# Two graph-attention layers on one core: k and q of layer 1 return together, and x is loaded later

## The chip, the cores and the metric

The kernel runs on one NeuronCore of a Trainium2 chip. TensorE (PE) multiplies matrices, VectorE (DVE), ScalarE (ACT) and GpSimd (POOL) do the elementwise work, and SyncE (SP) issues nearly all DMA transfers. The metric is the device time of one execution in microseconds; less is better. Nothing is split over cores, so the slowest core is the only core.

## The reference, cut to what matters

x is (128, 128, 512): 128 graphs of 128 nodes with 512 features; adj is a boolean mask (128, 128, 128). Two attention layers follow each other, each with a residual sum and a layer norm without scale. Layer 0 has 4 heads of 64, layer 1 has 8 heads of 64, a layer norm of its own input, and a mask in which every node also sees itself. All is float32.

```python
# layer 0
q, k, v = (split_heads(x @ W) for W in (Wq, Wk, Wv))            # 4 heads x 64
sim  = where(adj[:, None], einsum('bhid,bhjd->bhij', q, k) * scale, -finfo.max)
attn = softmax(sim)
x = layernorm(x + einsum('bhij,bhjd->bhid', attn, v) @ Wo + bo)
# layer 1
h = (x - mu) * rsqrt(var + 1e-5) * gamma + beta
q, k, v = split(h @ w_qkv.T)                                     # 8 heads x 64
scores = where(mask | eye, einsum('bihd,bjhd->bhij', q, k) * SCALE, -1e9)
out = einsum('bhij,bjhd->bihd', softmax(scores), v) @ w_out.T + b_out
x = layernorm(x + out)
```

## The kernel before

The 128 graphs are taken in 64 groups of two (`G = 2`). The function `step(s)` runs for s = 2 to 63; before it stands `opening()`, after it `closing_a`, `closing_b` (twice) and `last`. One step works on several groups at once: the projections of layer 0 for group s (`product_0`), the scores and softmax of layer 0 for group s-1 (part 0), attention and output of layer 0 for group s-2, the q, k and v of layer 1 for group s-3 (`qk`, `v`), scores and softmax of layer 1 for group s-4 (parts 1 and 2, one for each graph of the group), and attention and output of layer 1 for group s-5. Each matrix product is done in seven block products in place of eight (the numbers 1 to 7 in `product`, `product_0` and `out_product`), whose sums and differences DVE, ACT and POOL make.

The order on each engine is the order of the calls in `step`: the schedule is written by hand. Every engine takes its instructions in that order and waits in front of each one until its data and its buffer are ready. SP does the same with DMA transfers: a transfer that waits for something holds back all that were written after it.

Where a tile has to be transposed, DVE turns its blocks of 32 by 32 and the tile goes out to DRAM and comes back in four fetches (`fetch`, line 237), one for each quarter of the partitions, with the blocks in their new places. Five things take this way in each step:

- the normed rows of layer 0 on their way into layer 1: `turn` (store `scr`, line 234) and `arrive` (fetch into a tile with tag "raw"), read by ACT in `finish`;
- q and k of layer 0: `turn_qk0` (`scrqk`), `arrive_qk0` (`rawqk`); the q half is put in order by ACT in `q0_in_order` (line 277), and the k half is read by PE in the scores at line 562;
- the probabilities of each part: `blocks` (`scrp`, line 643) and `probs_arrive` (`pT`), read by PE in `attend` at line 691;
- k of layer 1: `taken_tokens` (lines 388 to 410). The half for the first graph comes from block product 2, the half for the second from product 4. Each is turned into the tile `tk`, which has one buffer, and stored at once (`scrk`, line 408). `k_arrive` fetches both halves into `kt`;
- q of layer 1: products 3 and 7 are turned into `tq`, which takes a turn of the tag "raw", and stored together (`scrq`, line 410). `q_arrive` fetches it into `rawq`, again with the tag "raw", and ACT puts it in order and scales it in `q_in_order` (line 435). PE reads `qo` and `kt` at line 568 in the next step.

Groups 0, 1 and the last three (`PLAIN_QK`) make q and k of layer 1 with the features on the partitions directly, and need no way through DRAM. The turned tiles of `turn`, `turn_qk0` and `blocks` share one tag "turned" with two buffers.

x is also loaded a second time, in a layout of 32-row quarters (`load_quarters`, four transfers, tile tag "x" with one buffer), which DVE turns in `transposed` (line 112). `load_ahead(s + 1)` (line 859) issues these four and the mask, near the beginning of the step; `arrive(s - 3)` follows it, and `flush()` issues, after ACT's layer norm, the store of the finished rows (`out_dram`, line 761).

The order of SP in one step of the steady part is therefore: x (4) and mask, raw (4), out, r, the stores of the probabilities of parts 0 and 1, scrqk, pT of parts 0 and 1 together (4), the first half of k, rawqk (4), the probabilities of part 2, q, the second half of k, rawq (4), kt (4), pT of part 2 (4), scr.

At the beginning, rows of the two weight matrices of layer 1 are loaded into tiles that are not used yet (`spare_rows`, lines 67 to 73), and transposed by PE.

Of the kernel before, what the change touches and what calls it, by code (L numbers as in the profile page):

```python
# [17 lines left out]
P = 128  # L18
D = 64
G = 2  # L20
# [7 lines left out]
def kernel(ctx: ExitStack, tc: tile.TileContext, x, adj, wq, wk, wv, wo, bo,  # L28
# [28 lines left out]
    def flush(what=later):  # L57
        while what:
            what.pop(0)()
# [7 lines left out]
    def spare_rows(pool, tag, n):  # L67
        rows_n = pool.tile([P, n, E], F32, tag=tag, name=f"raw_{tag}_{len(spare)}")
        spare.extend(rows_n[:, i] for i in range(n))

    for pool, tag, n in ((five, "r", 2), (five, "r", 2), (one, "kt", 2), (two, "v1", 2), (two, "v1", 2),
                         (one, "xT1", 2), (one, "aT1", 2), (one, "sm1", 2)):
        spare_rows(pool, tag, n)

    X, XT = {}, {}

    def load_rows(g):
        if 0 <= g < NG and g not in R:
            R[g] = five.tile([P, G, E], F32, tag="r", name=f"r_{g}")
            nc.sync.dma_start(R[g], x[g * G:(g + 1) * G].rearrange("b n e -> n b e"))  # L80
# [19 lines left out]
    def load_ahead(g):  # L100
        if g < NG:
            load_quarters(g)
            load_mask(g)
# [133 lines left out]
    def fetch(dst, scr):  # L237
        src = scr.rearrange("(a r) q x -> r q a x", r=32)
        for q in range(4):
            nc.sync.dma_start(dst[32 * q:32 * q + 32], src[:, q])  # L240
# [12 lines left out]
    def arrive(g):  # L253
        if not 0 <= g < NG:
            return
        RAW[1] = one.tile([P, 4, G, KC, 32], F32, tag="raw", name=f"raw_{g}")
        fetch(RAW[1].rearrange("p a b c i -> p a (b c i)"), SCR[1])

    PLAIN_0 = (0, 1, 2)
# [106 lines left out]
    def tap(kind, g, i, src, scale=1.0):  # L366
        EV[kind, i] = one.tile([P, 512], F32, tag=f"e{i}", name=f"e{kind}{i}_{g}")[:, :src.shape[1]]
        if scale == 1.0:
            nc.scalar.copy(EV[kind, i], src)  # L369
        else:  # L370
            nc.scalar.activation(EV[kind, i], src, AF.Copy, scale=scale)
# [11 lines left out]
        else:  # L383
            nc.vector.tensor_add(to, src, EV["v", e])

    QO, KT, TQ, SCRQ = {}, {}, {}, {}

    def taken_tokens(g, i, src):

        if i in (1, 5, 6):  # L390
            return tap("qk", g, i, src)
        if i == 4:
            done = src
        else:
            done = EV["qk", {2: 1, 3: 6, 7: 5}[i]]
            nc.vector.tensor_add(done, src, done)
        what, b = {2: ("k", 0), 7: ("q", 1), 3: ("q", 0), 4: ("k", 1)}[i]
        if i in (2, 7):
            SCRQ[what] = dram.tile([P, 4, G, K1 * 32], F32, tag=f"scr{what}", name=f"scr{what}_{g}")
        if i == 7:  # L400
            TQ[what] = one.tile([P, 4, G, K1 * 32], F32, tag="raw", name=f"tq_{g}")
        elif what == "k":
            TQ[what] = one.tile([P, 4, K1 * 32], F32, tag="tk", name=f"tk{b}_{g}")
        t = TQ[what] if what == "k" else TQ[what][:, :, b]
        nc.vector.transpose(t.rearrange("p q (c j) -> p q c j", j=32),
                            done.rearrange("p (c q j) -> p q c j", q=4, j=32))
        if what == "k":
            nc.sync.dma_start(SCRQ[what][:, :, b], t)
        elif i == 3:
            nc.sync.dma_start(SCRQ[what], TQ[what])  # L410

    def k_tile(g):
        KT[g] = one.tile([P, 4, G, K1, 32], F32, tag="kt", name=f"kt_{g}")
        return KT[g]

    def q_tile(g, b):
        QO[g, b] = one.tile([P, K1, N], F32, tag=f"qo{b}", name=f"qo{b}_{g}")
        return QO[g, b]

    def q_arrive(g):  # L420

        if 0 <= g < NG and g not in PLAIN_QK:
            RAW["q"] = one.tile([P, 4, G, K1, 32], F32, tag="raw", name=f"rawq_{g}")
            fetch(RAW["q"].rearrange("p a b c j -> p a (b c j)"), SCRQ["q"].rearrange("p q b x -> p q (b x)"))

    def k_arrive(g):

        if 0 <= g < NG and g not in PLAIN_QK:
            fetch(k_tile(g).rearrange("p a b c j -> p a (b c j)"), SCRQ["k"].rearrange("p q b x -> p q (b x)"))

    def q_in_order(g):

        if 0 <= g < NG and g not in PLAIN_QK:
            for b in range(G):
                nc.scalar.activation(q_tile(g, b).rearrange("p c (a j) -> p a c j", a=4), RAW["q"][:, :, b],
                                     AF.Copy, scale=SCALE)

    def plain_keys(g, b):
        return KT[g].rearrange("p a b c j -> p (a b c j)")[:, b * K1 * N:(b + 1) * K1 * N]

    def keys_of(g, b, kk, rows):
        if g in PLAIN_QK:
            return plain_keys(g, b).rearrange("p (c a j) -> p c a j", c=K1, a=4)[rows, kk]
        return KT[g][rows, :, b, kk]

    def taken_features(g, i, src):

        if i in (1, 5, 6):
            if i == 1:
                k_tile(g)  # L450
            return tap("qk", g, i, src, scale=SCALE if i != 1 else 1.0)
        if i == 2:
            nc.vector.tensor_add(plain_keys(g, 0), src, EV["qk", 1])
        elif i == 4:
            nc.scalar.copy(plain_keys(g, 1), src)
        else:
            b, e = {3: (0, 6), 7: (1, 5)}[i]
            nc.vector.scalar_tensor_tensor(q_tile(g, b).rearrange("p c n -> p (c n)"), src, SCALE,
                                           EV["qk", e], op0=ALU.mult, op1=ALU.add)
# [74 lines left out]


    SM, TOTAL, NMAX, PT, AT, SO = {}, {}, {}, {}, {}, {}
    K0, K1 = HEADS[0] // 2, HEADS[1] // 2
    PARTS = (0, 1, 2)

    def group_of(s, part):  # L540
# [3 lines left out]
    def scores(s, *parts):  # L544

        made = {}
        for part in parts or PARTS:
            g = group_of(s, part)
            if g is None:
                continue  # L550
            if part == 1:
                ps = [ps_st.tile([P, 512], F32, tag=t, name=f"sc{part}_{g}_{t}") for t in ("a0", "f0")]
            else:
                ps = [mm_tile(f"sc{part}_{g}_{i}") for i in range(2)]
            ps = [x.rearrange("p (k n) -> p k n", n=N) for x in ps]
            if part == 0:
                for b in range(G):
                    for h in range(HEADS[0]):
                        r = slice((h % 2) * D, (h % 2 + 1) * D)
                        k_ = (qkv0[r, b, h // 2, 2].rearrange("p (a j) -> p a j", j=32) if g in PLAIN_0 else  # L560
                              RAW[0][r, :, 1, b * K0 + h // 2])
                        nc.tensor.matmul(ps[h % 2][:, b * K0 + h // 2, :].rearrange("p (a j) -> p a j", j=32),  # L562
                                         qkv0[r, b, h // 2, 1], k_, start=True, stop=True)
            else:
                b = part - 1
                for h in range(HEADS[1]):
                    r = slice((h % 2) * D, (h % 2 + 1) * D)
                    nc.tensor.matmul(ps[h % 2][:, h // 2, :].rearrange("p (a j) -> p a j", j=32),  # L568
                                     QO[g, b][r, h // 2], keys_of(g, b, h // 2, r), start=True, stop=True)
            made[part] = ps  # L570
        return made

# [33 lines left out]
    def exps(s, part, *halves):  # L606
        if group_of(s, part) is None:
            return
        sm, nmax, total = SM[part], NMAX[part], TOTAL[part]
        for i in halves:  # L610
            for k in range(K1):
                nc.scalar.activation(sm[:, i, k, :], sm[:, i, k, :], AF.Exp, bias=nmax[:, i, k:k + 1],  # L612
                                     accum_out=total[:, i, k:k + 1])
# [193 lines left out]
    def qk(g, *which):  # L807
        for i in which:
            product("qk", g, i)
# [46 lines left out]
    def step(s):  # L856

        made = scores(s)
        load_ahead(s + 1)
        if s > 3:  # L860
            sums(0, s)
            arrive(s - 3)
        flush()
        load_rows(s - 1)
        masked(made, s, 0, 1, 2)
        if s == 3:
# [30 lines left out]
        product_0(s, 7)  # L897
        finish(s - 3, 1)
        exps(s, 2, 1)
        blocks(s, 1)  # L900
        product_0(s, 3)
        if s == 3:
# [9 lines left out]
            prepare(1)  # L912
        flush()
        if s > 2:
            probs_arrive(s, 0, 1)
        qk(s - 3, 2)
        arrive_qk0(s)
        blocks(s, 2)
        qk(s - 3, 6)
        if s == 3:  # L920
            weight_sums(w1v, wsv, 0)
# [7 lines left out]
        if s == 3:  # L929
            weight_sums(w1v, wsv, 1)  # L930
        qk(s - 3, 3, 4)
        q_arrive(s - 3)
        k_arrive(s - 3)
        probs_arrive(s, 2)
        out_product(1, s - 5, 1, 2)
        if s in (3, 4):
# [9 lines left out]
        out_product(1, s - 5, 6, 5)  # L946
        v(s - 3, 5)
        out_product(1, s - 5, 7, 3, 4)
        q_in_order(s - 3)
        q0_in_order(s)  # L950
        addend(0, s - 1)
        v(s - 3, 7)
        stats(1, s - 5, 0)
# [194 lines left out]
```

## Time and profile before

| | us |
|---|---|
| timed runs, median of 3 | 2765.82 (2763.13 to 2767.58) |
| the profiled execution | 2759.03 |
| its span, from the first to the last instruction | 2757.3 |
| median time from issue to landing: store of q (`scrq`) / half of k (`scrk`) | 5.0 / 5.8 |
| fetches of q (`rawq`) / k (`kt`), each of 128 KB | 2.9 / 3.5 |
| fetches of pT for two parts (256 KB) / for one (128 KB) | 5.2 / 3.9 |
| fetches of rawqk / of x | 6.1 / 5.0 |

The granted TensorE clock was 0.999 in the mean. DMA moved 562.73 MB in all, 204 GB/s in the mean. A page of a profile gives the busy time of each engine (PEld is the weight load of TensorE, which lies beside its matmuls), the same in 40 slices as tenths, and the groups of instructions with their mean duration. A wait is named by the engine that stood, its line and tile, and by what ended it. In the timeline a line is: start, duration, engine, line, operation, written tile <- read tiles, how many; and in brackets the idle time ahead of it and who ended it. SPq is SP's queue of DMA issues: the duration there is that of the issue, not of the transfer.

### The profile page before, as it was taken

The page shows a single profiled execution, that of the slowest core. Times are in us where ns is not written, and L with a number is a line of the kernel's source. Part 1 is how long each engine was busy: PE and PEld are TensorE (multiplying, and loading weights), DVE is VectorE, ACT ScalarE, POOL GpSimd, SP SyncE. Part 2 cuts the span into 40 slices and gives each one's busy share as a digit, 9 for nine tenths or more (in the row PEclk, how much of TensorE's full clock was granted, in tenths as well). Part 3 has the DMA queues.
Part 4 walks back from the last instruction along what each step waited for, and adds up shares of the span by engine and source line. Part 5 has one row for each costly group of instructions (what it writes and reads, how often), then busy time and mean ns, then how long its engine had stood idle before and what let it go on. Part 6 is the DMA issues. An engine that isn't in the chain of part 4 may idle for free.

```text
span 2757.3 us, 49223 instructions
## 1 busy us (share of the span) xinstructions
PE 2725.2 (99%) x15781; PEld 2024.6 (73%) x15781; DVE 2025.0 (73%) x3662; ACT 1510.6 (55%) x4805; POOL 1750.2 (63%) x2311
## 2 busy tenths in 40 slices
PE   8999999999999999999999999999999999999998
PEld 7867777677776677776776766777767767677787
DVE  5777777777777777777777777777777777777665
ACT  3465565564564655655645546556556465465554
POOL 4566666666666666666666666666666666666664
PEclk9999999999999999999999999999999999999999
DMA  6577878778778788787787787877877877878741
GB/s 171 151 196 211 220 205 222 209 205 225 214 202 227 202 215 218 206 220 213 202 228 209 208 224 203 218 212 207 225 207 207 225 206 214 219 204 222 204 126 62
DMA packets 525330, 562.73 MB, mean 204 GB/s; under 512 B 55304, under 2 KB 434192, under 8 KB 525072
## 3 DMA queue, kind: packets, MB, share of 16 engines
q1 hardware_dynamic: 524496, 559.05, 75.8%
q8 instruction: 127, 2.08, 0.3%
q14 instruction: 131, 1.07, 0.1%
q10 hardware_dynamic: 576, 0.52, 0.1%
HBM read 300.95 MB, written 258.47 MB: 203 GB/s over the span
## 4 chain that ended last, share of the span: by engine, by line
PE 89%; DMA 4%; ACT 3%; DVE 1%; POOL 1%; SPq 1%; issue 1%; ACTq 0%; POOLq 0%; DVEq 0%
PE qka L359 14%; PE a L490 11%; PE oa L528 11%; PE va L359 8%; PE qkf L359 7%; PE av L691 6%; PE of L528 6%; PE f L490 5%; PE vf L359 4%; PE qkc L359 4%; PE c L490 3%; PE oc L528 3%; PE sc L562 2%; PE sc L568 2%; PE vc L359 2%; DMA scrk<-tk 2%
## 5 line engine op out<-in xcount | busy, mean ns | idle before, releaser
L612 ACT ACTIVATE sm<-sm,nmax 128x128 f32<-128x128 f32 x1536 | 595.4, 393 | 7.6 <-DVE nmax L603 6.0
L621 POOL TENSOR_TENSOR sm<-sm,rec 128x1024 f32<-128x1024 f32 x192 | 364.1, 1896 | 360.5 <-DVE rec L620 357.6
L713 POOL TENSOR_TENSOR r<-r,bias 128x1024 f32<-128x1024 f32 x128 | 301.4, 2356 | 127.1 <-ACT r L712 127.1
L532 DVE TENSOR_TENSOR r<-oa,r 128x256 f32<-128x256 f32 x508 | 211.5, 416 | 159.8 <-PE oa L528 126.0
L612 ACT ACTIVATION_READ_ACCUMULATOR sm<-sm,nmax 128x1 f32 x1536 | 295.4, 192 | 0.0
L369 ACT COPY ev<-va 128x256 f32<-128x256 f32 x128 | 47.6, 372 | 442.9 <-PE va L359 442.9
L732 POOL TENSOR_SCALAR ve<-mv 128x2 f32<-128x2 f32 x191 | 41.4, 217 | 376.8 <-DVE mv L725 366.3
L639 DVE STREAM_TRANSPOSE turnedp<-sm 128x1024 f32<-128x1024 f32 x188 | 233.4, 1242 | 63.8 <-POOL sm L621 63.8
L758 ACT ACTIVATE r<-r,shift,root 128x512 f32<-128x512 f32 x254 | 192.8, 808 | 122.2 <-POOL shift L747 122.2
L603 DVE TENSOR_REDUCE nmax<-sm 128x8 f32<-128x1024 f32 x192 | 226.3, 1204 | 0.1
L359 PE MATMUL qkf<-w,xs 128*128 128x512 f32 x472 | 221.8, 592 | 0.0
L359 PE MATMUL qka<-wsqk,xs 128*128 128x512 f32 x472 | 221.8, 592 | 0.0
L528 PE MATMUL oa<-wso,so 128*128 128x256 f32 x760 | 206.1, 380 | 2.3 <-POOL so L323 1.8
L528 PE MATMUL of<-wo,so 128*128 128x256 f32 x760 | 206.0, 380 | 0.7 <-POOL so L323 0.4
L323 POOL TENSOR_TENSOR xs<-xT 128x256 f32<-128x256 f32 x256 | 188.3, 736 | 28.3 <-DVE xT L112 23.4
L490 PE MATMUL a<-ws,xs 128*128 128x128 f32 (+1 forms) x760 | 182.1, 375 | 0.0
L490 PE MATMUL f<-w,xs 128*128 128x128 f32 (+1 forms) x760 | 182.1, 375 | 0.0
L597 DVE COPY_PREDICATED sm<-m,sc 128x512 f32<-128x512 uint8 x256 | 172.5, 727 | 12.1 <-PE sc L562 3.6
L724 DVE BATCH_NORM_STATS2 st<-r 128x6 f32<-128x512 f32 x254 | 174.9, 688 | 2.3
L583 POOL MEMSET sm<- 128x1024 f32 x192 | 174.9, 952 | 0.0
L359 PEld LDWEIGHTS qka<-wsqk,xs 128*128 128x128 f32 x472 | 89.7, 190 | 112.9 <-issue 112.9
L359 PEld LDWEIGHTS qkf<-w,xs 128*128 128x128 f32 x472 | 89.7, 190 | 112.9 <-issue 112.9
(181 smaller groups left out, 6478.6 us busy)
## 6 DMA issues: line engine op xcount, KB each, us to landing
scrp<-turnedp SPq DMA_DIRECT2D x188, 512.0 KB, 3.2
pT<-scrp SPq DMA_DIRECT2D x252, 256.0 KB, 5.2
x<-in_x_dram SPq DMA_DIRECT2D x256, 128.0 KB, 5.0
r<-in_x_dram SPq DMA_DIRECT2D x64, 512.0 KB, 3.2
out_dram<-r SPq DMA_DIRECT2D x63, 512.0 KB, 4.3
scr<-turned SPq DMA_DIRECT2D x62, 512.0 KB, 4.7
raw<-scr SPq DMA_DIRECT2D x248, 128.0 KB, 4.1
pT<-scrp SPq DMA_DIRECT2D x248, 128.0 KB, 3.9
```

The source lines that it names most:

```text
L323: nc.gpsimd.tensor_tensor(o, a0, a1, op=op)
L359: nc.tensor.matmul(o, lhsT, rhs, start=first and m == 0, stop=m == len(todo) - 1, skip_group_check=True)
L490: nc.tensor.matmul(o, lhsT, rhs, start=first and n == 0, stop=n == len(todo) - 1, skip_group_check=True)
L528: nc.tensor.matmul(acc, left[:, c], right[:, c], start=first and c == 0, stop=c == hk - 1, skip_group_check=True)
L532: nc.vector.tensor_add(part, acc, part)
L583: nc.gpsimd.memset(sm, NEG1 if part else NEG0)
L603: nc.vector.tensor_reduce(NMAX[part], SM[part], AX.X, ALU.max, negate=True)
L612: nc.scalar.activation(sm[:, i, k, :], sm[:, i, k, :], AF.Exp, bias=nmax[:, i, k:k + 1], accum_out=total[:, i, k:k + 1])
L621: nc.gpsimd.tensor_tensor(SM[part], SM[part], rec[:, :, :, None].to_broadcast([P, 2, K1, N]), op=ALU.mult)
L639: nc.vector.transpose(t.rearrange("p q (h r) -> p q h r", r=32), SM.pop(part).rearrange("p i k (q r) -> p q (i k) r", r=32))
L713: nc.gpsimd.tensor_tensor(R[g], R[g], (bias0, bias1)[l][:, None, :].to_broadcast([P, G, E]), op=ALU.add)
L758: nc.scalar.activation(R[g][:, b], R[g][:, b], AF.Identity, bias=shift[:, b:b + 1], scale=root[:, b:b + 1])
```

## The change

Layer 1's k and q now share one DRAM scratch and one lasting tile `KQ`, which holds for each quarter first k and then q. They are fetched together by `kq_arrive` in four transfers of 256 KB, where `q_arrive` and `k_arrive` issued four of 128 KB each. The q half of `KQ` is also the place into which `arrive` fetches the normed rows (before: tag "raw"), and the k half is where the plain groups write k. k is turned into one tile for both halves, with the tag "x" (before: `tk`, one tile for each half, one buffer); q is turned into a tile of the tag "turned" (before: "raw"). Both halves of k are still stored one by one, q at once.

In `step`, four calls move. `load_ahead(s + 1)` goes behind `arrive(s - 3)` and `flush()`. `probs_arrive` for part 0 goes ahead of `blocks(s, 1)`, and part 1 is fetched alone in the old place. `arrive_qk0(s)` goes behind `blocks(s, 2)`. `q0_in_order(s)` goes ahead of `q_in_order(s - 3)`. The weight rows at the beginning use `KQ` in place of two other tiles.

SP's order in one step becomes: raw (4), out, x (4) and mask, r, the probabilities of part 0, pT of part 0 (4), the probabilities of part 1, scrqk, pT of part 1 (4), the first half of k, the probabilities of part 2, rawqk (4), q, the second half of k, kq (4), pT of part 2 (4), scr.

```diff
--- before.py
+++ after.py
@@ -68,9 +68,15 @@
         rows_n = pool.tile([P, n, E], F32, tag=tag, name=f"raw_{tag}_{len(spare)}")
         spare.extend(rows_n[:, i] for i in range(n))
 
-    for pool, tag, n in ((five, "r", 2), (five, "r", 2), (one, "kt", 2), (two, "v1", 2), (two, "v1", 2),
-                         (one, "xT1", 2), (one, "aT1", 2), (one, "sm1", 2)):
-        spare_rows(pool, tag, n)
+    K0, K1 = HEADS[0] // 2, HEADS[1] // 2
+    KQ = const.tile([P, 4, 2, G, K1, 32], F32, name="kq")
+
+    spare_rows(five, "r", 2)
+    spare_rows(five, "r", 2)
+    kq_rows = KQ.rearrange("p a w b c j -> p (a w b c j)")
+    spare.extend(kq_rows[:, i * E:(i + 1) * E] for i in range(4))
+    for pool, tag in ((two, "v1"), (two, "v1"), (one, "xT1"), (one, "aT1")):
+        spare_rows(pool, tag, 2)
 
     X, XT = {}, {}
 
@@ -253,7 +259,7 @@
     def arrive(g):
         if not 0 <= g < NG:
             return
-        RAW[1] = one.tile([P, 4, G, KC, 32], F32, tag="raw", name=f"raw_{g}")
+        RAW[1] = KQ[:, :, 1]
         fetch(RAW[1].rearrange("p a b c i -> p a (b c i)"), SCR[1])
 
     PLAIN_0 = (0, 1, 2)
@@ -383,7 +389,7 @@
         else:
             nc.vector.tensor_add(to, src, EV["v", e])
 
-    QO, KT, TQ, SCRQ = {}, {}, {}, {}
+    QO, TQ, SCRQ = {}, {}, {}
 
     def taken_tokens(g, i, src):
 
@@ -395,64 +401,48 @@
             done = EV["qk", {2: 1, 3: 6, 7: 5}[i]]
             nc.vector.tensor_add(done, src, done)
         what, b = {2: ("k", 0), 7: ("q", 1), 3: ("q", 0), 4: ("k", 1)}[i]
-        if i in (2, 7):
-            SCRQ[what] = dram.tile([P, 4, G, K1 * 32], F32, tag=f"scr{what}", name=f"scr{what}_{g}")
+        if i == 2:
+            SCRQ[g] = dram.tile([P, 4, 2, G, K1 * 32], F32, tag="scrkq", name=f"scrkq_{g}")
+            TQ["k"] = one.tile([P, 4, G, K1 * 32], F32, tag="x", name=f"tk_{g}")
         if i == 7:
-            TQ[what] = one.tile([P, 4, G, K1 * 32], F32, tag="raw", name=f"tq_{g}")
-        elif what == "k":
-            TQ[what] = one.tile([P, 4, K1 * 32], F32, tag="tk", name=f"tk{b}_{g}")
-        t = TQ[what] if what == "k" else TQ[what][:, :, b]
+            TQ["q"] = one.tile([P, 4, G, K1 * 32], F32, tag="turned", bufs=2, name=f"tq_{g}")
+        t = TQ[what][:, :, b]
         nc.vector.transpose(t.rearrange("p q (c j) -> p q c j", j=32),
                             done.rearrange("p (c q j) -> p q c j", q=4, j=32))
         if what == "k":
-            nc.sync.dma_start(SCRQ[what][:, :, b], t)
+            nc.sync.dma_start(SCRQ[g][:, :, 0, b], t)
         elif i == 3:
-            nc.sync.dma_start(SCRQ[what], TQ[what])
-
-    def k_tile(g):
-        KT[g] = one.tile([P, 4, G, K1, 32], F32, tag="kt", name=f"kt_{g}")
-        return KT[g]
+            nc.sync.dma_start(SCRQ[g][:, :, 1], TQ["q"])
 
     def q_tile(g, b):
         QO[g, b] = one.tile([P, K1, N], F32, tag=f"qo{b}", name=f"qo{b}_{g}")
         return QO[g, b]
 
-    def q_arrive(g):
+    def kq_arrive(g):
 
         if 0 <= g < NG and g not in PLAIN_QK:
-            RAW["q"] = one.tile([P, 4, G, K1, 32], F32, tag="raw", name=f"rawq_{g}")
-            fetch(RAW["q"].rearrange("p a b c j -> p a (b c j)"), SCRQ["q"].rearrange("p q b x -> p q (b x)"))
-
-    def k_arrive(g):
-
-        if 0 <= g < NG and g not in PLAIN_QK:
-            fetch(k_tile(g).rearrange("p a b c j -> p a (b c j)"), SCRQ["k"].rearrange("p q b x -> p q (b x)"))
+            fetch(KQ.rearrange("p a w b c j -> p a (w b c j)"), SCRQ.pop(g).rearrange("p q w b x -> p q (w b x)"))
 
     def q_in_order(g):
 
         if 0 <= g < NG and g not in PLAIN_QK:
             for b in range(G):
-                nc.scalar.activation(q_tile(g, b).rearrange("p c (a j) -> p a c j", a=4), RAW["q"][:, :, b],
+                nc.scalar.activation(q_tile(g, b).rearrange("p c (a j) -> p a c j", a=4), KQ[:, :, 1, b],
                                      AF.Copy, scale=SCALE)
 
-    def plain_keys(g, b):
-        return KT[g].rearrange("p a b c j -> p (a b c j)")[:, b * K1 * N:(b + 1) * K1 * N]
-
-    def keys_of(g, b, kk, rows):
-        if g in PLAIN_QK:
-            return plain_keys(g, b).rearrange("p (c a j) -> p c a j", c=K1, a=4)[rows, kk]
-        return KT[g][rows, :, b, kk]
+    def plain_keys(b):
+        return KQ[:, :, 0, b].rearrange("p a c j -> p c a j")
 
     def taken_features(g, i, src):
 
         if i in (1, 5, 6):
-            if i == 1:
-                k_tile(g)
             return tap("qk", g, i, src, scale=SCALE if i != 1 else 1.0)
+        by_block = "p (c a j) -> p c a j"
         if i == 2:
-            nc.vector.tensor_add(plain_keys(g, 0), src, EV["qk", 1])
+            nc.vector.tensor_add(plain_keys(0), src.rearrange(by_block, a=4, j=32),
+                                 EV["qk", 1].rearrange(by_block, a=4, j=32))
         elif i == 4:
-            nc.scalar.copy(plain_keys(g, 1), src)
+            nc.scalar.copy(plain_keys(1), src.rearrange(by_block, a=4, j=32))
         else:
             b, e = {3: (0, 6), 7: (1, 5)}[i]
             nc.vector.scalar_tensor_tensor(q_tile(g, b).rearrange("p c n -> p (c n)"), src, SCALE,
@@ -534,7 +524,6 @@
 
 
     SM, TOTAL, NMAX, PT, AT, SO = {}, {}, {}, {}, {}, {}
-    K0, K1 = HEADS[0] // 2, HEADS[1] // 2
     PARTS = (0, 1, 2)
 
     def group_of(s, part):
@@ -566,7 +555,7 @@
                 for h in range(HEADS[1]):
                     r = slice((h % 2) * D, (h % 2 + 1) * D)
                     nc.tensor.matmul(ps[h % 2][:, h // 2, :].rearrange("p (a j) -> p a j", j=32),
-                                     QO[g, b][r, h // 2], keys_of(g, b, h // 2, r), start=True, stop=True)
+                                     QO[g, b][r, h // 2], KQ[r, :, 0, b, h // 2], start=True, stop=True)
             made[part] = ps
         return made
 
@@ -856,11 +845,11 @@
     def step(s):
 
         made = scores(s)
-        load_ahead(s + 1)
         if s > 3:
             sums(0, s)
             arrive(s - 3)
         flush()
+        load_ahead(s + 1)
         load_rows(s - 1)
         masked(made, s, 0, 1, 2)
         if s == 3:
@@ -897,6 +886,8 @@
         product_0(s, 7)
         finish(s - 3, 1)
         exps(s, 2, 1)
+        if s > 2:
+            probs_arrive(s, 0)
         blocks(s, 1)
         product_0(s, 3)
         if s == 3:
@@ -912,10 +903,10 @@
             prepare(1)
         flush()
         if s > 2:
-            probs_arrive(s, 0, 1)
+            probs_arrive(s, 1)
         qk(s - 3, 2)
+        blocks(s, 2)
         arrive_qk0(s)
-        blocks(s, 2)
         qk(s - 3, 6)
         if s == 3:
             weight_sums(w1v, wsv, 0)
@@ -929,8 +920,7 @@
         if s == 3:
             weight_sums(w1v, wsv, 1)
         qk(s - 3, 3, 4)
-        q_arrive(s - 3)
-        k_arrive(s - 3)
+        kq_arrive(s - 3)
         probs_arrive(s, 2)
         out_product(1, s - 5, 1, 2)
         if s in (3, 4):
@@ -946,8 +936,8 @@
         out_product(1, s - 5, 6, 5)
         v(s - 3, 5)
         out_product(1, s - 5, 7, 3, 4)
+        q0_in_order(s)
         q_in_order(s - 3)
-        q0_in_order(s)
         addend(0, s - 1)
         v(s - 3, 7)
         stats(1, s - 5, 0)
```

## The prediction

> **What bounds the kernel now.** I read the page's busy times and slices first, then the waits by total, then the timelines of PE, DVE and SP over one step, last the DMA share in short windows.
>
> ```profile
> span 2757.3 us, 49223 instructions
> PE 2725.2 (99%) x15781; PEld 2024.6 (73%) x15781; DVE 2025.0 (73%) x3662; ACT 1510.6 (55%) x4805; POOL 1750.2 (63%) x2311
> PE   8999999999999999999999999999999999999998
> ```
>
> TensorE has work in every slice. A busy PE need not be a PE at its pace, so I measured the step: from the first score matmul of one step to that of the next it is 42.00 or 42.14 us (by the parity of the group), and between equal landmarks the matmuls start at equal distances to 0.02 us. Only a few steps are longer, up to 42.9. So there is no slack to win in a plain step; the change can take away the irregular pieces, or add new ones.
>
> The waits (engine and line, what it waited for, total us, times, longest):
>
> ```profile
> ACT qo L435 <- DMA rawq<-scrq: 133.8, 59, 3.6
> ...
> DVE tk L405 <- DMA scrk<-tk: 19.4, 22, 1.7
> ...
> PEld va L359 <- DVE tk L405: 6.2, 10, 0.9
> ...
> PEld sc L562 <- ACT qkv L277: 4.9, 12, 1.0
> ```
>
> The first is large but ACT has room there. The second is the single tile tk: the second half of k can't be turned until the first half's store has landed, and until it is turned the PSUM bank of va is not free. Here is a step where that store took 7.5 us (1337.85 to 1345.4):
>
> ```profile
> 1345.41 0.72 DVE L405 STREAM_TRANSPOSE tk<-qka 128x512 f32<-128x512 f32 x1 [1.67 <-DMA scrk<-tk]
> ...
> 1346.18 1.13 PE L359 MATMUL va<-w,xT 128*128 128x256 f32 x4 [0.47 <-DVE tk L405]
> ```
>
> SP's queue over the end of an ordinary step, whose successor's scores start at 1313.86 (layer 0), with those of layer 1 at 1314.86:
>
> ```profile
> 1293.36 2.15 SPq L240 DMA_DIRECT2D pT<-scrp  x4
> 1295.60 0.52 SPq L408 DMA_DIRECT2D scrk<-tk  x1
> 1296.17 2.20 SPq L240 DMA_DIRECT2D rawqk<-scrqk  x4
> 1298.85 0.52 SPq L643 DMA_DIRECT2D scrp<-turnedp  x1
> 1301.46 0.34 SPq L410 DMA_DIRECT2D scrq<-tq  x1
> 1303.28 0.52 SPq L408 DMA_DIRECT2D scrk<-tk  x1
> 1306.97 1.73 SPq L240 DMA_DIRECT2D rawq<-scrq  x4
> 1308.80 1.80 SPq L240 DMA_DIRECT2D kt<-scrk  x4
> 1310.64 1.86 SPq L240 DMA_DIRECT2D pT<-scrp  x4
> ```
>
> And the DMA engines in windows (next to last column: their share):
>
> ```profile
> 1294.00:1307.00 13.00, 13.00 (x43) 7.84 (x42) 7.72 (x12) 3.14 (x6) 10.54 (x14) 1.00 1.04 274
> 1308.00:1322.00 14.00, 14.00 (x137) 12.43 (x136) 10.66 (x20) 7.43 (x19) 6.82 (x13) 1.00 1.07 235
> 1331.00:1333.00 2.00, 2.00 (x10) 1.33 (x9) 2.00 (x4) 2.00 (x9) 1.77 (x4) 1.00 0.00 0
> ```
>
> The DMA engines are full where k and q go out and come back, and idle earlier in the step. That decides this case: q and k come back only 1 to 3 us before PE reads them.
>
> **What the Trainium skill says.** "DMA: Bandwidth & Descriptors", Anatomy of one DMA: DMA engines wait on no semaphore; the issuing sequencer does, before dispatch. The trace agrees: rawq's first fetch stands at SP until 1306.97, about when q's store (issued 1301.46, median 5.0 us) has landed, and all behind it stands too. Same page, Queues, rings and completion order: descriptors are taken in ring order, so a store issued behind loads pays for their backlog. Here the second half of k took 4.3 us in the full stretch, scrqk in a quiet one 2.9. "Perfetto Trace Analysis", DMA Optimizations: transfers under 2 KB carry overhead; both directions of this occur below and I price them alike.
>
> **The change part by part.** Counts of PE, ACT, DVE and POOL instructions stay as they are; per step SP still issues 39 DMAs (k and q 4 fetches instead of 8, probabilities 12 instead of 8).
>
> *k turned into x's tile.* The wait for the first half's store goes. x's tile is free by then (the DVE turned it itself, just before), and the next x is issued long after the second store has landed. Gain on PE, by the landmarks of all steps: eight steps lose 0.18 to 0.63 us ahead of va, 3.7 in sum, and some ten more lose about 0.1: together 4.8. Next in line there is the end of qk's last product, which is there in plain steps too.
>
> *q's turned tile in the ring "turned".* Six tiles a step through two buffers, was five. Part 2's probabilities (DVE 1294.97) then wait for part 1's store, as before; that store moves later, see below. q's tile waits for scrqk's store, landed 1295.8, needed 1299.07; the next turn waits for part 2's store, landed 3 us ahead. Cost 0.
>
> *Layer 0's probabilities alone.* Four fetches of 128 KB (1.86 us of SP, by the pT row) go ahead of part 1's store. SP stands from 1286.2 until part 0's store has landed (3.2 us after 1285.70: 1288.9), ends at 1290.8; part 1's store leaves then and not at 1289.63. It lands at about 1294, 1 us before the DVE needs its buffer; if late, DVE has 2.13 us idle after the part 2 turn (before 1298.35). Cost 0, at most some tenths. scrqk (1292.85) is not touched. In return 0.5 MB are moved in a stretch where the DMA engines were idle.
>
> *Part 2's store ahead of rawqk's four fetches.* Store 1.5 to 2.4 us earlier, the fetch (2.20 us of SP) about 1 us later, landing some 10 us before its reader. Cost 0.
>
> *k and q in four fetches.* The fetch now waits for both stores. Before, 3.0 MB were issued from 1293.36 to 1303.28, the last landing at 1307.6. With 0.5 MB less, at 274 GB/s, the queue is through 1.9 us earlier: 1305.7. (Floor: second k turned at 1301.7, stored at 1302.45, plus 2.9: 1305.4.) q and k together took 6.6 us from the first fetch at 1306.97 to the last landing (1310.2 plus 3.4); so both are there at 1312.3, where before q was there at 1311.4 and k at 1313.6. ACT puts q in order in 1.15: 1313.5, for PE at 1314.86. Slack 1.4 us. ACT's copy of v behind it starts at 1313.97 anyway. Bounds: 1311 (floor and a fetch of 5.6) and 1316.0 (no earlier store, and the 8.4 us that 1 MB of pT took in the full stretch). I take 1312.3. pT's part 2 follows at about 1308, 2.6 us earlier than now.
>
> *q0_in_order ahead of q_in_order.* 0.60 us of ACT whose data are long there. Layer 0's scores no longer wait behind q: one stall of 0.59 (at 217.29) and small ones of 0.2: gain 1.0.
>
> *x and the mask later.* Five DMAs, 2.83 us of SP, go behind raw's four fetches and the out store. The out store waits for ACT's norm (ends 1318.0), so x leaves at about 1318.6 and lands near 1326, for the DVE at 1332; r's load, which waits for the out store to land (about 1323), is not delayed. Raw comes 1 to 2 us earlier. Cost 0. In the closing, PE stands 0.96 us at 2630.5 for raw; it comes at least that much earlier: gain 1.0.
>
> *KQ as one lasting tile.* Raw in the q half waits for q_in_order, as the shared tag did; plain groups write the same bytes in runs of 32. Cost 0.
>
> Sum: 4.8 + 1.0 + 1.0 = 6.8 us off. The profiled execution took 2759.03 (span 2757.3), which would become 2752.2. The median shown is 2765.82, 6.8 above it; taken from that: **2759.0**.
>
> **The rivals.** (a) Slower: k's second store lands as late as before (1307.6) and the joint fetch takes 7.0, so q is there at 1314.6 and the first scores of layer 1 can start 0.62 later at 1315.3, half a us late, in each of 59 steps: +30 us, 2796. For it: the first q copy now also waits for k; against it: 0.5 MB less in the queue. It decides from a landing later than 1314.2 on, 1.9 us after my estimate. (b) Hardly any effect: the stalls at va go, but DMA jitter (every tenth step or so a store is 1 to 2 us late) now meets the joint fetch and puts as much back: a gain of 0 to 5, 2763. For it: k was up to 1.7 late in such steps. (c) More gain: timed runs lie 4 to 8.6 us over the profiled one; if that is the same store waits, they go too: 2752. No view shows them.
>
> **How the numbers follow.** Forecast 0.45 (2756 to 2762), (c) 0.14, (b) 0.23, (a) 0.18 (2772 to 2815). 0.2%, 5.5 us, is what a measurement here can tell: faster is below 2760.3. That is (c) and seven tenths of the forecast: 0.46; slower is (a), 0.18; the rest 0.36. Range 2750 to 2772: (c) to the foot of (a), leaving out most of (a).
>
> **What would show it.** DVE's tk has no wait for a store; va starts 1.73 us after oa in all steps; kq's first fetch leaves about 1.3 us earlier relative to the scores than rawq did; ACT's q copy ends before the layer 0 scores do; x lands 6 us before it is turned. Wrong if score matmuls wait for qo or kq in most steps, if part 1's store makes DVE late, or if steps get longer than 42.14.

## The result, and the profile after

| | before | after |
|---|---|---|
| timed runs, median of 6, us | 2765.98 (2763.13 to 2769.26) | 2756.67 (2755.74 to 2756.92) |
| the profiled execution, us | 2759.03 | 2756.88 |
| its span, us | 2757.3 | 2755.1 |
| DMA packets of SP's queue | 524496 | 547728 |
| their time, share of 16 engines | 75.8% | 71.6% |

The ratio is 0.9966, with a 95% interval of 0.9954 to 0.9977: 9.3 us less, where 6.8 were forecast. The two profiled executions differ by only 2.2 us. The one of before was quicker than every timed run of it, the one of after lies among its own; so the profile shown in the prediction held fewer losses than a usual execution. A second profile of before, below, fills that gap. The timed runs of after also lie closer together: 1.2 us where before has 6.1.

First the page of the changed kernel:

```profile
span 2755.1 us, 49293 instructions
PE 2725.6 (99%) x15781; PEld 2027.5 (74%) x15781; DVE 2026.3 (74%) x3662; ACT 1505.7 (55%) x4805; POOL 1753.5 (64%) x2311
```

TensorE does the same work. Then its waits (engine, line and tile, what ended the wait; us in total, times, longest), the rows that answer to those shown of before:

```profile
ACT qo L430 <- DMA kq<-scrkq: 228.2, 59, 5.2
...
DVE tk L410 <- PE qka L365: 16.5, 59, 0.3
...
PEld sc L551 <- ACT qo L430: 5.3, 16, 0.3
...
PEld sc_a L557 <- ACT qo L430: 1.7, 4, 0.7
```

DVE's turn of k's second half waits only for the product it turns, 0.3 us each time; the store is out of it, and so is the wait of va. ACT's q copy waits longer than before (228.2 for 133.8 us), and a new row stands at the bottom: the scores of layer 1 (`sc_a`) wait for that copy. The row of L551 above it is no such loss: the weight loads of the layer 0 scores stand 0.3 us in every step, and where nothing else ends that gap it is called "issue" (14.8 us, 45 times). This is SP's queue over the end of one step, whose successor's layer 0 scores start at 1312.53:

```profile
1293.57 1.89 SPq L246 DMA_DIRECT2D pT<-scrp  x4
1295.57 0.53 SPq L413 DMA_DIRECT2D scrkq<-tk  x1
1296.19 0.61 SPq L632 DMA_DIRECT2D scrp<-turnedp  x1
1296.85 2.88 SPq L246 DMA_DIRECT2D rawqk<-scrqk  x4
1300.30 0.52 SPq L415 DMA_DIRECT2D scrkq<-tq  x1
1301.30 0.52 SPq L413 DMA_DIRECT2D scrkq<-tk  x1
1304.59 1.73 SPq L246 DMA_DIRECT2D kq<-scrkq  x4
1306.37 1.85 SPq L246 DMA_DIRECT2D pT<-scrp  x4
1308.75 0.34 SPq L240 DMA_DIRECT2D scr<-turned  x1
1315.42 1.74 SPq L246 DMA_DIRECT2D kq<-scr  x4
1317.27 0.40 SPq L750 DMA_DIRECT2D out_dram<-r  x1
1317.71 2.52 SPq L104 DMA_DIRECT2D x<-in_x_dram  x4
```

The joint fetch leaves 7.94 us ahead of those scores; before, q's fetch left 6.89 ahead of them. ACT's timeline of the same moment shows what that is worth:

```profile
1312.17 1.15 ACT L430 ACTIVATE qo<-kq 128x512 f32<-128x512 f32 x2 [3.82 <-DMA kq<-scrkq]
```

The copy starts 0.36 us ahead of the layer 0 scores, and the scores of layer 1, which read it, come 1.0 us after those. Both copies end 0.8 us after the layer 0 scores start, 0.2 ahead of that; the first half alone, which is read first, has 0.7 us to spare. Before, q's copy started 2.4 us ahead in this place. In a few steps this is not enough; the worst one in PE's timeline:

```profile
218.16 0.37 PE L557 MATMUL sc_a<-kq,qo 64*128 64x128 f32 x1 [0.54 <-ACT qo L430]
```

Lengths of steps, from one step's layer 0 scores to the next, are 42.00 or 42.14 us wherever nothing stands. Over 55 steps of the steady part they sum to 2319.8 us in the first profile of before and to 2317.3 after. In the last stage after gives back 1.3 us, from 130.9 to 132.2 between the last such scores and the end. The wait of 0.96 us for raw is gone from it, and about 2.4 us come in around the last fetch of probabilities (PE timelines, first after, then before):

```profile
2722.39 3.39 PE L680 MATMUL av<-pT,v 128*64 128x128 f32 x32 [2.29 <-DMA pT<-scrp]
```

```profile
2726.20 1.97 PE L691 MATMUL av<-pT,v 128*64 128x128 f32 x32 [1.50 <-DMA pT<-scrp]
```

The wait is 0.8 us longer, and the matmuls behind it take 3.39 us for 1.97. The view by windows shows why these are slow (after; the third number from the end is the granted clock of TensorE):

```profile
2700.00:2722.00 22.00, 19.24 (x164) 18.16 (x164) 11.83 (x23) 7.79 (x22) 11.68 (x15) 1.00 0.35 97
2723.00:2724.00 1.00, 1.00 (x13) 1.00 (x11) 0.00 (x0) 0.00 (x0) 0.65 (x1) 0.50 0.00 0
2727.00:2740.00 13.00, 12.97 (x73) 10.76 (x73) 8.26 (x18) 8.21 (x31) 6.14 (x6) 1.00 0.11 42
```

For 3.4 us behind this wait the clock was 0.50; before, it was 1.00 in this place.

### The profile page after: what moved, and what is told of

Its sections match the earlier page's. It is cut to its first block, busy times and chain, and to the rows that moved or that the text cites. A ratio compares the mean times of both kernels' runs of the same rounds, so it can differ in the third digit from the quotient of the medians.

```text
span 2755.1 us, 49293 instructions
## 1 busy us (share of the span) xinstructions
PE 2725.6 (99%) x15781; PEld 2027.5 (74%) x15781; DVE 2026.3 (74%) x3662; ACT 1505.7 (55%) x4805; POOL 1753.5 (64%) x2311
## 3 DMA queue, kind: packets, MB, share of 16 engines
q1 hardware_dynamic: 547728, 559.05, 71.6%
## 4 chain that ended last, share of the span: by engine, by line
PE 95%; DMA 2%; POOL 1%; ACT 1%; DVE 1%; issue 0%; SPq 0%; ACTq 0%; POOLq 0%; DVEq 0%
PE qka L365 16%; PE a L480 12%; PE oa L518 11%; PE qkf L365 8%; PE va L365 8%; PE av L680 6%; PE f L480 6%; PE of L518 6%; PE qkc L365 4%; PE vf L365 4%; PE c L480 3%; PE oc L518 3%; PE sc L551 2%; PE sc L557 2%; PE vc L365 2%; PE sc_a L557 2%
## 5 line engine op out<-in xcount | busy, mean ns | idle before, releaser
L430 ACT ACTIVATE qo<-kq 128x512 f32<-128x512 f32 x118 | 67.9, 622 | 228.2 <-DMA kq<-scrkq 228.2
```

## The experiments

All times stand beside runs of the kernel before on the same chip; three chips were used, and its median there was 2764.0 to 2767.6, so the ratio is the better measure where two runs come from different chips.

**Where a usual execution of before loses its time.** The kernel before, unchanged, profiled once more.

> The kernel before once more, for a second profile: its profiled execution took 2759.03 where its timed runs take 2763 to 2769. Theory (the timed runs hold more of the same store waits): an execution of 2763 to 2769 shows 12 to 20 steps that lose time ahead of va, 8 to 12 us in sum. Rival: the surplus lies elsewhere, in the first or last stages or in the scores, and va's losses stay at about 5 us.

This execution took 2766.83 us. Its waits:

```profile
DVE tk L405 <- DMA scrk<-tk: 28.5, 32, 1.8
...
PEld sc L562 <- ACT qkv L277: 9.4, 16, 1.0
PEld va L359 <- DVE tk L405: 9.4, 12, 1.0
```

All three have grown against the first profile (19.4, 4.9 and 6.2). By the landmarks of the steps, twelve lose 0.12 to 0.79 us ahead of va and 0.1 each on the product behind it: 7.8 in sum, a little under the forecast of 8 to 12. Eleven steps lose 0.15 to 0.70 ahead of the layer 0 scores, 4.1 in sum, because ACT puts layer 0's q in order behind layer 1's, which comes late. 0.7 us go in the scores of layer 1 where k is late. The theory was half right: the surplus of the timed runs is the same kind of wait, but both kinds of it, and the second grew most (first profile: about 1 us).

**Only the second half of k apart.**

```diff
-            TQ[what] = one.tile([P, 4, K1 * 32], F32, tag="tk", name=f"tk{b}_{g}")
+            TQ[what] = one.tile([P, 4, K1 * 32], F32, tag="x" if b else "tk", name=f"tk{b}_{g}")
```

> The kernel before, with only the second half of k turned into x's tile. Theory (the wait for tk's store was the main loss): DVE's second turn of k never waits for a store, va starts 1.73 us after oa in every step, and the time falls by 5 to 8 us, to 2758 to 2761, the larger part of the 9.3 us of the whole change. Rival (the gain comes from the order of q and q0 or from the emptier DMA queue): the wait goes, but the time falls by less than 3 us, 2763 or more.

2759.19 us, ratio 0.9971 (0.9961 to 0.9982), 8.4 us less. DVE's row for tk is the same as that of the changed kernel, and no step loses anything ahead of va. What stays is the other wait:

```profile
PEld sc L562 <- ACT qkv L277: 11.3, 24, 1.0
```

**Both waits away, nothing else.** The edit above, and layer 0's q put in order first.

```diff
-        q_in_order(s - 3)
         q0_in_order(s)
+        q_in_order(s - 3)
```

> The kernel before, with the second half of k turned into x's tile and layer 0's q put in order ahead of layer 1's; no joint fetch, no lasting tile, no moved loads. Theory (these two waits are all that the change wins): the layer 0 scores lose nothing to q0, the only losses left are steps with a late k, and the time is within 1.5 us of the changed kernel's in this comparison, 9 to 12 us below the kernel before. Rival (the emptier queue and the joint fetch bring a part of their own): it stays 2 us or more above the changed kernel.

2757.05 us, ratio 0.9967 (0.9954 to 0.9979), where the changed kernel beside it took 2756.42, ratio 0.9965 (0.9953 to 0.9978):

> The changed kernel as it is, beside the others on one chip: 9 to 12 us below the kernel before; the mark for the other three.

Two lines do what the whole change does, within what can be told apart. Six steps still lose 0.15 to 0.63 us in the scores of layer 1, 2.2 in sum, where k is late; the execution that was profiled took 2755.22, the lowest of the five, so a usual one may lose more. The joint fetch, the lasting tile and the moved loads bring nothing on balance. That does not say that each of them brings nothing, and the next run shows that one brings a good deal.

**Only the probabilities apart.** The kernel before, with part 0 fetched ahead of `blocks(s, 1)` and part 1 alone in the old place; k's tile is still one, ACT's order the old one.

```diff
+        if s > 2:
+            probs_arrive(s, 0)
         blocks(s, 1)
...
-            probs_arrive(s, 0, 1)
+            probs_arrive(s, 1)
```

> The kernel before, with the probabilities of parts 0 and 1 fetched apart, part 0 early, and nothing else. Theory (both waits have one root, the full DMA queue behind the 1 MB of probabilities): the first half of k lands in about 3 us and not 6, so DVE never stands for tk although the tile is still one; q's store lands 1.5 us earlier, so layer 0's scores do not wait for q0 although ACT's order is the old one; 2755 to 2759. Rival (the wait for tk needs a second buffer): va still loses time in ten steps or so, and less than half of the gain is there, 2763 or more.

2751.79 us, ratio 0.9949 (0.9935 to 0.9962): 14.0 us less than before and 4.6 less than the whole change, below the range expected, with nothing changed but where the probabilities are fetched. Its waits:

```profile
ACT qo L435 <- DMA rawq<-scrq: 29.7, 42, 1.8
PEld sc L562 <- issue: 20.1, 61, 0.3
DVE tk L405 <- PE qka L359: 16.5, 59, 0.3
```

DVE never stands for the store although tk has one buffer, and the layer 0 scores never wait for q0 although ACT's order is the old one: their 0.3 us is the plain one in all 61 cases. Its queue on SP (layer 0 scores of the next step at 1310.86):

```profile
1286.14 1.74 SPq L240 DMA_DIRECT2D pT<-scrp  x4
...
1291.45 1.75 SPq L240 DMA_DIRECT2D pT<-scrp  x4
1293.30 0.52 SPq L408 DMA_DIRECT2D scrk<-tk  x1
...
1298.63 0.34 SPq L410 DMA_DIRECT2D scrq<-tq  x1
1299.63 0.53 SPq L408 DMA_DIRECT2D scrk<-tk  x1
1302.05 1.73 SPq L240 DMA_DIRECT2D rawq<-scrq  x4
1303.89 1.97 SPq L240 DMA_DIRECT2D kt<-scrk  x4
```

In the median of the steps, the first half of k lands 3.1 us after its issue (before: 6.1), q's store 3.2 (5.0), the second half of k 3.0 (4.5). So q's fetch leaves 8.9 us ahead of the scores and not 7.2, ACT's copy starts 4.4 us ahead, and all but one of the steady steps have their bare length. Both waits had one root: the 1 MB of probabilities that stood in the DMA queue in front of these stores. This run splits that fetch and moves one part of it early; whether the split alone would do was not run.

**The same fetch undone in the changed kernel.** Parts 0 and 1 fetched together, the rest of the change in place.

> The changed kernel, with the probabilities of parts 0 and 1 fetched together in the old place. Theory (the lone fetch of part 0 is what lets k and q come back in time, as it takes 0.5 MB out of the full stretch): k's second store lands about 1.5 us later, ACT's first q copy starts about 1.2 us after the scores of layer 0 start, the first scores of layer 1 stand 0.5 to 1.2 us in nearly every step, and the time is 2785 to 2825. Rival (the queue was not what held k's store; its own latency was): the joint fetch leaves within 0.4 us of the changed kernel's and the time stays within 5 us of 2757.

2830.32 us, ratio 1.0228 (1.0214 to 1.0242), 62.8 us more than before, 5 us beyond the range expected. The waits:

```profile
ACT qo L430 <- DMA kq<-scrkq: 328.0, 59, 6.4
PEld sc_a L557 <- ACT qo L430: 65.1, 55, 2.3
PE sc_a L557 <- ACT qo L430: 53.9, 51, 1.9
```

The second half of k lands 4.9 us after its issue where the changed kernel has 3.2; the joint fetch leaves 6.2 us ahead of the scores, not 7.9, and the q copy starts 1.3 after them. The 55 steps take 2386.0 us for 2317.3, 1.25 more each. The joint fetch can be borne only behind the lone one.

**q and k apart, q first.** The changed kernel with two fetches of the shared scratch.

```diff
-            fetch(KQ.rearrange("p a w b c j -> p a (w b c j)"), SCRQ.pop(g).rearrange("p q w b x -> p q (w b x)"))
+            scr = SCRQ.pop(g)
+            for w in (1, 0):
+                fetch(KQ[:, :, w].rearrange("p a b c j -> p a (b c j)"), scr[:, :, w].rearrange("p q b x -> p q (b x)"))
```

> The changed kernel, with q and k fetched apart from the shared scratch, four fetches each, q first; nothing else moves. Theory (the joint fetch spends nearly all the slack of q: its copy starts 0.3 us before the scores, and in five steps it is late by 0.2 to 0.7 us): q leaves when its own store has landed, its copy on ACT starts 4 us or more ahead of the scores, the stalls of the layer 1 scores go or shrink to those where k is late, and the time is 1 to 2 us below the changed kernel's in this comparison. Rival (the joint fetch is worth its saving of 4 issues, and k then lands later): k is late instead, and the time is the same as the changed kernel's or up to 10 us above it.

2751.76 us, ratio 0.9949 (0.9936 to 0.9961), 4.7 us below the changed kernel beside it. The gain is above the 1 to 2 expected. SP spends more on it (layer 0 scores at 1310.72; the joint fetch took 1.73):

```profile
1302.08 3.80 SPq L246 DMA_DIRECT2D kq<-scrkq  x8
```

In the median step it leaves 8.9 us ahead of the scores, and the copy starts 4.2 ahead. No steady step loses anything: 2314.0 us over the 55 steps against 2317.3, which is 3.3; the last stage is 1.7 shorter (130.5 for 132.2), at the last fetch of probabilities. In both profiles of the changed kernel PE waited over 2 us there (2.29 and 2.18, here 1.71), and the granted clock was 0.50 for the next 3.4 us; here it stayed at 1.00. So the 4.7 us are not all the price of the joint fetch. What brings the clock down is open: with x in its old place, below, PE waited as long in this place and the clock stayed up.

**x in its old place.** First in the changed kernel, then together with q first. `load_ahead(s + 1)` goes back in front of `arrive(s - 3)`.

> The changed kernel, with x and the mask loaded in the old place, near the start of the step, ahead of raw. Theory (moving x costs and brings nothing in the steady part, since it stands behind k, q and the probabilities in the queue either way): 2755 to 2759. Rival (x ahead of raw takes SP and the DMA engines where raw and the probabilities of part 2 land): raw or the av products wait, and the time is 2762 or more.

2755.40 us, ratio 0.9958 (0.9946 to 0.9971): not to be told from the changed kernel (0.9966, 0.9954 to 0.9977).

> The changed kernel with q and k fetched apart, q first, and x and the mask in the old place. Theory (with q early nothing in the steady part is near its limit, and x's place is worth nothing): 2751 to 2753, as with q first alone. Rival (x in front of raw costs time that the score stalls of the joint fetch hid, or brings some): 2755 or more, or below 2750.

2751.68 us, ratio 0.9957 (0.9945 to 0.9970); with q first alone it was 2751.76 and 0.9949 (0.9936 to 0.9961) on another chip. x's place is worth nothing that could be told apart here.

**The joint fetch behind part 2's probabilities.**

```diff
-        kq_arrive(s - 3)
         probs_arrive(s, 2)
+        kq_arrive(s - 3)
```

> The changed kernel with the joint fetch put behind the fetch of part 2's probabilities: 0.5 MB more ahead of q and k in the queue. Theory (q has 0.2 to 0.3 us of slack, and beyond it each us of a later landing is a us of each step): the landing is about 2.6 us later, ACT's first q copy starts about 2.3 us after the scores of layer 0, the layer 1 scores stand 1.9 us a step, and the time is 2850 to 2885. Rival (the stall draws the later work out and the next step's stores come out of the full stretch, so it does not add up): under 2830.

2777.79 us, ratio 1.0053 (1.0037 to 1.0068). Slower, but far less than expected. The queue (layer 0 scores of that step start some 8 us after the joint fetch):

```profile
1308.62 0.52 SPq L415 DMA_DIRECT2D scrkq<-tq  x1
1309.62 0.52 SPq L413 DMA_DIRECT2D scrkq<-tk  x1
1310.23 2.44 SPq L246 DMA_DIRECT2D pT<-scrp  x4
1313.45 1.87 SPq L246 DMA_DIRECT2D kq<-scrkq  x4
```

The probabilities go out while SP would have stood for k's store anyway, so the joint fetch leaves only 0.2 us later and its data stand behind a queue that has partly drained: the copy starts 0.8 us later than in the changed kernel, at 0.4 after the scores, and steps stand 0 to 1.2 us (2334.7 us over the 55, 0.3 more each). I had put the whole 0.5 MB ahead of q, as if both left at the same moment.

## Why the prediction was right

**The bound.** Right: TensorE's work is the same, plain steps keep 42.00 and 42.14 us, and all that was won is irregular standing. The bare steps of the best run sum to 2314.0, so a usual execution of before (2326.4) had 12.4 us to win in the 55 steps.

**k turned into x's tile, gain 4.8.** The mechanism is right (the tile alone took all of it away), the size was that of a lucky execution: 7.8 in the second profile. The "ten more" steps that lose about 0.1 are the same steps, which lose it on the product behind va; the sum of 4.8 stands. The prediction saw that its profile lay 6.8 under the median and left the gap to a rival, the one in which timed runs hold more of the same waits. That rival was right about where the gap lies.

**Layer 0's q first, gain 1.0.** Same: 4.1 in the second profile.

**The joint fetch, taken as free with 1.4 us of slack.** This is the term that was mis-sized on the other side. k's second store landed when the step said (fetch at 7.9 us ahead of the scores, worked out 8.2). But the fetch took 7.6 us from its first issue to the q copy, where 6.6 had been worked out from an issue and a median landing; before's own record of that step has 6.9 (1306.97 to 1313.86). So by the prediction's measure (the end of both copies against the scores of layer 1) the slack was 0.2 and not 1.4. Eight steps lose 0.1 to 0.9 us there, and with smaller pieces about 3 of the 3.3 us over bare length go this way; q first wins them back. Over the 55 steps 12.4 us were won and 3.3 given back, which is the 9.1 between the two kernels. The rival in which late stores meet the joint fetch and give something back was right in kind; it returned about a quarter and not all.

**The slower rival.** Its mechanism and its point of decision hold. The first half of the copy takes 0.62 us, and the scores of layer 1 come 1.0 after those of layer 0, so a copy that starts later than 0.38 makes them stand. By the medians and the 55 steps: with the copy at -0.34, 0.06 us a step over bare length; at 0.4, 0.4; at 1.3, 1.3 (more than the median's excess, since single steps lie later than the median). What kept it off is the lone fetch of part 0, and its price without that was 63 us above before, twice the 30 put on it.

**The lone fetch, cost 0.** Right as a cost, but its worth was missed. The prediction counted its 0.5 MB only for the time at which the joint fetch can leave, and did not carry it back to k's first store, five lines higher in the same queue. That store was the one that DVE stood for. Had the landing been worked out again for every store behind the moved fetch, it would have shown that the tile and ACT's order on one side and the lone fetch on the other remove the same losses, so that the first two are spare beside the third.

**x and the mask later, cost 0.** Right, both ways. x lands 11.8 us after the scores, 6.6 ahead of its turn. Raw leaves only about 0.5 us earlier than before and not 1 to 2: scr's store is issued earlier, but takes 6.7 us to land where it took 4.7. The closing's 0.96 us for raw went as forecast; 2.4 us came in around the last fetch of probabilities, a longer wait and a stretch at half clock, which the prediction did not have.

**The total.** The forecast of 6.8 and the 9.3 measured lie close through luck in part: the irregular waits were put at 5.8 where those of a usual execution were 12.4 in the 55 steps, while the price of the joint fetch (3.3) and the longer stand at the last fetch of probabilities (2.4) were not in the sum. Errors of opposite sign nearly cancelled.

## What to carry to other kernels

Where a store and a fetch stand in one DMA queue, a wait for a buffer may be a wait for the queue: before giving it a second buffer, look at what was issued ahead of the store, and move a large fetch into a stretch in which the DMA engines are idle. Joining two fetches makes the first reader wait for the later producer; count the slack of the earlier one, and fetch it apart if its consumer has work to do on it first. One profiled execution that lies under all timed runs is a lucky one: price irregular waits from one near the median.

## What the runs showed of the hardware

The same store of 256 KB, the first half of k, took 6.1 us to land in the median behind a fetch of 1 MB and 3.0 to 3.1 us behind one of 0.5 MB begun 1 to 1.5 us later in the step, with the other 0.5 MB some 5 us ahead of that. With both fetches joined again in the changed kernel it took 6.1.

The time of the packets, as a share of 16 engines, was not set by their number, for equal bytes: 75.8% with 524496 packets before, 73.4% with the lone fetch alone (559056), 71.6% in the changed kernel (547728) and 73.4% in the same kernel with x back in its old place (547728), 70.3% with q first (581712). The prediction left the overhead of small transfers out on both sides; no cost of it shows here. That packets take longer where many transfers meet would fit these figures, but no run separates it.

The granted TensorE clock was 0.50 for 3.4 us behind PE's wait of 2.3 us near the end of the changed kernel, and 1.00 behind a wait of 2.4 us in the run with x in its old place. What decides between the two is not shown.
